# Layer 0 attention: Q, K and the negated maximum in two float32r parts, one product per head pair and key tile

## The chip, the cores and the metric

The kernel runs on one core of a Trainium2 chip. The metric is the device time of one execution in microseconds (us), lower is better. In the profile PE is the matrix engine (TensorE), PEld its loading of the stationary operand, DVE the vector engine, ACT the scalar engine, POOL the GpSimd engine and SP the engine whose queue issues most transfers. A "product" below is one matmul instruction.

## The reference

Two transformer layers follow each other; the second reads the first one's result. Only the attention of layer 0 is changed. It has 32 heads of 8 elements on 8 key/value heads, 2 batches of 1024 tokens, and a causal mask:

```
q = rope(x @ Wq + bq)      # 32 heads, 8 elements each
k = rope(x @ Wk + bk)      # 8 heads, each used by 4 query heads
v = x @ Wv + bv
scores = einsum('bhqd,bhkd->bhqk', q, k) / sqrt(8)
scores = where(kpos > qpos, -inf, scores)
out = (softmax(scores) @ v) @ Wo + bo
```

Everything is float32. The feed-forward net of layer 0 (8-bit arithmetic), then a windowed attention and a feed-forward net with ternary weights in layer 1 complete the program.

## The kernel before

**Tiling.** A query tile (b, i) is 128 tokens of batch b; there are 16 of them, done in the order (0,0) to (0,7), then (1,7) down to (1,0). Heads are split in two halves e = 0, 1: half 0 lives on partitions from 0, half 1 on partitions from 64, and the products of the two halves are issued as a pair, one right after the other.

**Float32 by bfloat16 parts.** Each q and each k is cut into three bfloat16 parts (`split`, lines 821 to 846: ACT rounds, DVE or POOL subtracts, twice). Of the nine pairs of parts, eight are stacked along the contraction, 8 pairs times 8 elements = 64 rows (`qmain`, `kmain`); the ninth pair stands with three rows for the parts of the negated maximum in a second stack of 35 rows (`qlast`, `klast`). In the trace, `k0` of batch 0 appears as plain `k`. The parts are written to a scratch in DRAM (`qscr`, `kscr`) and read back row by row into the stacks: `load_q` (line 940) issues eight transfers per query tile on SP, `stacks` (line 898) eight per chunk of 512 keys.

**Two passes over the scores.** For every query tile the kernel first finds the row maximum, and then computes the transposed scores with the maximum already subtracted:

- `max_unit` (lines 990 to 1034) multiplies the 64-row stacks (line 1016, tile `m`), up to 512 keys wide, adds the causal mask by bfloat16 products with an identity on 64 rows (line 988), and lets DVE reduce (line 1028, tile `mx`). Its three PSUM buffers hold one and a half such pairs. There are 304 units.
- `take_max` (lines 1036 to 1047) cuts the maximum into three parts on DVE, `turn_max` transposes them on PE, copies on ACT and sends them through DRAM (`mscr`) into the last three rows of the query stack.
- `weigh` (line 1075) forms the shifted scores `s` of a head pair and key tile with two products per half, the 64-row stack and the 35-row stack, accumulated:

```
for n, height in enumerate((HALF, EXTRA)):
    for e in range(2):
        rows = slice(HALF * e, HALF * e + height)
        nc.tensor.matmul(sc[e], kst[b][n][rows, ...], qst[b, i][n][rows, ...],
                         start=n == 0, stop=n == 1)
```

  ACT takes the exponential (line 1090). There are 288 such steps. `gather` (line 1110) multiplies the weights with v: four products of 9 columns in float32 (tile `acc`), once for every two steps.

**Order.** PE's order is the order of recording. The loop at the end of `attention0` counts slots: each slot records about one `max_unit` for a later tile, pieces of the feed-forward net of layer 0 and of other preparations as they come due, then one `weigh`, and after every second one the `gather` of the group before. The other engines' queues are ordered by the scheduler of the framework. The start is a chain: project K and Q for the first 512 tokens (`project`, line 853), cut them, write the scratch, load the stacks tile by tile (the next tile's write is issued behind the loads of the tile before), then the rest of the rope table and other inputs, all on SP. A fixed number of idle products (`keep_busy`, line 144) stands ahead of the first units. The parts of K for batch 1 share their memory with a staging area for the weights of the feed-forward net (`spare`), those of batch 0 later hold weights of layer 1.

## Time and profile before

Three executions took 1162.53, 1162.91 and 1166.25 us, a median of 1162.91 us. The profiled execution spans 1163.5 us from its first to its last instruction, 0.6 us from that median, so durations from the profile are set against the median as they are.

| stretch, us | what runs | PE busy | DVE busy | ACT busy | granted clock |
|---|---|---|---|---|---|
| 0 to 43 | first projections, cutting, first stacks | 29.68 | 27.78 | 9.15 | 0.92 |
| 43 to 94 | maxima of the first tiles, stacks of tiles 1 to 3 | 31.20 | 32.80 | 4.06 | 0.67 |
| 94 to 130 | first weighing | 30.54 | 28.32 | 15.50 | 0.81 |
| 130 to 400 | layer 0 | 226.59 | 232.48 | 145.01 | 0.91 |
| 400 to 770 | layer 0 | 329.85 | 299.91 | 257.40 | 0.96 |
| 770 to 1163.5 | layer 1 | 356.69 | 168.65 | 156.98 | 0.94 |

A stretch's busy time of an engine is the time in which at least one of its instructions was running by the trace. Products overlap each other, and the end of a product in the trace is modelled, so a busy PE is not a full PE. The chain of waits is the work followed back from the last instruction, each time to what released it.

### The profile page before, as it was taken

Reading aid. Unit: us, or ns where it says so; the run is one execution under the profiler, and the core shown is the slowest. Engines: PE = TensorE matmul, PEld = TensorE weight load, DVE = VectorE, ACT = ScalarE, POOL = GpSimd, SP = SyncE. Lnnn points to the kernel's source line nnn. Section 1 sums busy time; section 2 is a strip of 40 time slices with the busy share of each in tenths; the row PEclk is TensorE's granted clock in tenths of the full one; section 3 lists DMA queues with packets and bytes.
Section 4 is the critical chain, followed back from the end, with each engine's and each line's share of the span. In section 5 each row is a group of like instructions: output and inputs, shape, how many; then the busy total and the mean of one; then the engine's idle time right before and its main releaser. Section 6 shows DMA issues by size and latency. Waiting matters only on the chain.

```text
span 1163.5 us, 19952 instructions
## 1 busy us (share of the span) xinstructions
PE 1004.6 (86%) x7660; PEld 483.1 (42%) x7699; DVE 789.9 (68%) x1476; ACT 588.1 (51%) x1061; POOL 402.5 (35%) x440
## 2 busy tenths in 40 slices
PE   5758786888888989897989999896999999998897
PEld 2333331222332322232223333323567667666576
DVE  7467989889687998789897888703555544533431
ACT  2003461765356756576766777762463534533431
POOL 2007223424126121312133335545654635513400
PEclk9767896999799989998999999998999989989998
DMA  5432101000101010100001000006811332431200
GB/s 177 116 105 73 51 1 40 17 26 31 55 11 41 15 28 10 25 22 5 24 3 26 22 14 24 2 3 82 110 44 39 60 83 47 82 62 33 39 20 20
DMA packets 65928, 49.05 MB, mean 42 GB/s; under 512 B 20904, under 2 KB 59432, under 8 KB 65832
## 3 DMA queue, kind: packets, MB, share of 16 engines
q1 hardware_dynamic: 60632, 39.05, 15.1%
q0 software_dynamic: 4112, 8.26, 2.9%
q8 instruction: 60, 0.98, 0.4%
q10 hardware_dynamic: 1088, 0.46, 0.1%
q14 instruction: 36, 0.29, 0.1%
HBM read 34.12 MB, written 15.20 MB: 42 GB/s over the span
## 4 chain that ended last, share of the span: by engine, by line
PE 50%; DVE 28%; DMA 8%; ACT 6%; POOL 3%; issue 3%; SPq 2%; DVEq 0%; ACTq 0%; POOLq 0%
DVE mx L1028 14%; PE acc L1110 8%; PE s L1080 7%; PE f1gu L676 4%; PE sk L555 4%; PE f1o L715 3%; PE m L1016 3%; PE pqk L469 3%; PE sq L520 2%; DMA qscr<-ptq 2%; PE gu L305 2%; DMA qkv<-all 2%; ACT p L1090 2%; DMA qs<-mscr 1%; PE m L988 1%
## 5 line engine op out<-in xcount | busy, mean ns | idle before, releaser
L1028 DVE TENSOR_REDUCE mx<-m 128x1 f32<-128x512 f32 (+3 forms) x608 | 372.4, 653 | 95.8 <-PE m L1016 54.6
L1090 ACT ACTIVATE p<-s 128x512 f32<-128x512 f32 x576 | 307.2, 606 | 133.5 <-PE s L1080 131.0
L1110 PE MATMUL acc<-p,v 128*9 128x512 f32 x1152 | 171.0, 615 | 1.8 <-ACT p L1090 1.2
L1016 PE MATMUL m<-k,qmain 64*128 64x512 bf16 (+3 forms) x384 | 94.9, 359 | 52.9 <-DVE mx L1028 40.4
L1094 POOL TENSOR_SCALAR_AFFINE_SELECT p<-p 128x512 f32<-128x512 f32 x128 | 83.5, 675 | 160.8 <-ACT p L1090 160.5
L1016 PE MATMUL m<-kmain,qmain 64*128 64x512 bf16 (+3 forms) x384 | 83.1, 333 | 24.8 <-DVE mx L1028 22.7
L1016 PEld LDWEIGHTS <-qmain 64*128 64x128 bf16 x768 | 50.4, 100 | 81.8 <-issue 52.4
L988 PEld LDWEIGHTS <-ident_h 64*128 64x128 bf16 x832 | 45.6, 98 | 89.6 <-issue 67.0
L988 PE MATMUL m<-mask_q,ident_h 64*128 64x128 bf16 (+3 forms) x832 | 75.5, 223 | 2.4 <-DVE mx L1028 2.2
L1080 PE MATMUL s<-qmain,k 64*128 64x512 bf16 x288 | 68.1, 398 | 9.0 <-ACT ob L275 3.1
L1080 PE MATMUL s<-qmain,kmain 64*128 64x512 bf16 x288 | 64.2, 389 | 5.3 <-ACT p L1090 2.6
L1080 PE MATMUL s<-qlast,k 35*128 35x512 bf16 x288 | 63.9, 392 | 0.0
L1080 PEld LDWEIGHTS <-k 64*128 64x128 bf16 (+1 forms) x576 | 21.0, 95 | 99.0 <-issue 90.9
L1080 PE MATMUL s<-qlast,klast 35*128 35x512 bf16 x288 | 61.2, 387 | 0.0
L685 DVE SCALAR_TENSOR_TENSOR h<-h,f1gu 128x512 f32<-128x512 f32 x32 | 21.9, 686 | 49.2 <-ACT h L684 49.2
L676 PEld LDWEIGHTS <-wgu_bf 128*128 128x128 bf16 x384 | 38.1, 100 | 41.4 <-issue 4.7
L690 POOL TENSOR_TENSOR sq<-h 128x512 f32<-128x512 f32 x28 | 29.1, 1040 | 69.4 <-DVE h L686 68.0
L555 PE MATMUL sk<-qs,ks 25*128 25x128 f32 x512 | 45.5, 422 | 7.7 <-DMA qs<-mscr 7.7
L1153 POOL TENSOR_TENSOR x<-x,aos 128x256 f32<-128x256 f32 x16 | 11.9, 746 | 116.0 <-ACT aos L1152 116.0
L563 ACT ACTIVATE p<-sk 128x2048 f32<-128x2048 f32 x16 | 30.0, 1877 | 41.1 <-PE sk L555 41.1
L528 DVE TENSOR_REDUCE m<-sq 128x16 f32<-128x2048 f32 x16 | 36.6, 2286 | 20.9 <-PE sq L520 20.9
L153 POOL TENSOR_TENSOR hp<-hrest,hp 128x512 bf16<-128x512 f32 x32 | 37.0, 1157 | 35.4 <-ACT hp L152 35.4
(290 smaller groups left out, 1809.0 us busy)
## 6 DMA issues: line engine op xcount, KB each, us to landing
qmain<-qscr SPq DMA_DIRECT2D x64, 96.0 KB
qkv<-all SPq DMA_DIRECT2D x16, 384.0 KB
qscr<-ptq POOLq DMA_DIRECT2D x6, 384.0 KB, 4.2
x<-in_x SPq DMA_DIRECT2D x16, 128.0 KB
qmain<-qscr SPq DMA_DIRECT2D x32, 64.0 KB
qs<-qkv SPq DMA_DIRECT2D x16, 128.0 KB
ks<-qkv SPq DMA_DIRECT2D x16, 128.0 KB
vs<-qkv SPq DMA_DIRECT2D x16, 128.0 KB
```

The source lines that it names most:

```text
L153: engines[1].tensor_tensor(parts[2], r, parts[1], ALU.subtract)
L469: nc.tensor.matmul(pqk, x[k], wqk[:, k, :], start=(k == 0), stop=(k == 1))
L528: last(nc.vector.tensor_reduce(m, ps, AX.X, ALU.max, negate=True))
L555: nc.tensor.matmul(ps[:, s, r, :], columns(k, slice(S * s, S * s + HD + 9), 4 * b + r), columns(q, slice(S * s, S * s + HD + 9), 4 * b + r ...
L676: nc.tensor.matmul(ps[g], wgu_bf[:, k, g * HID + hc * P : g * HID + (hc + 1) * P], x_parts[n][m][:, k, :], start=(k == 0 and m == 0), stop ...
L988: nc.tensor.matmul(out[e][:, :, lo:], ident_h[rows, t, :], rhs.to_broadcast([HALF, out[e].shape[1], P - lo]), start=start and t == 0, stop ...
L1016: nc.tensor.matmul(sc[e][:, s * width : (s + 1) * width], qst[b, i][0][rows, p, :], kst[b][0][rows, lo // 512, p // 4, 0:width], start=not ...
L1028: reduced = nc.vector.tensor_reduce(mx[b, i][:, part, e, pairs[0] : pairs[0] + n], sc[e][:, : n * width].rearrange("p (s k) -> p s k", s=n ...
L1080: nc.tensor.matmul(sc[e], kst[b][n][rows, j // 4, u, j % 4 * P : (j % 4 + 1) * P], qst[b, i][n][rows, 4 * u : 4 * u + 4, :], start=n == 0, ...
L1090: nc.scalar.activation(p, sc[e], AF.Exp, scale=scale)
L1094: nc.gpsimd.affine_select(out=by_head, in_=by_head, compare_op=ALU.is_ge, fill=0.0, base=0, pattern=[[0, 4], [1, P]], channel_multiplier=-1,)
L1110: nc.tensor.matmul(acc[32 * s : 32 * s + HD0 + 1, :], vst[b][:, j, 4 * G + s, :], ps[s], start=(j == 0), stop=(j == i),)
```

## The change

Q and K are cut into two parts instead of three, kept in float32 and multiplied as float32r. The four pairs of parts make one stack of 4 times 8 = 32 rows; two rows more hold the parts of the negated maximum, so that `weigh` is one product of 34 rows per half, where it was two. `max_unit` uses the first 32 rows. A stack now takes four transfers instead of eight, with rows of 8 KB instead of 4 KB. The maximum is transposed in float32, cut by ACT (rounding) and DVE (rest, from PSUM), and sent as two rows. The tiles `qlast` and their clearing go; `klast` and its clearing give way to clearing both stacks of K with ones. Memory of K for batch 0 is taken over for layer 1 by new tiles (`take_k0`, called at the same place where the weights of layer 1 are loaded). A float32r product carries the loading of its stationary operand with it; a bfloat16 one has a separate instruction for that. The core of the diff:

```
 HALF = 64
-AUG = 32
-EXTRA = AUG + 3
+STACK = 32
+FULL = STACK + 2
...
-    k0 = [cp.tile([P, 2, KV0 // 2, 512], BF, tag=f"k0{n}", name=f"k0_{n}") for n in range(2)]
+    k0 = [cp.tile([P, KV0 // 2, 512], FR, tag=f"k0{c}", name=f"k0_{c}") for c in range(2)]
...
             def split(...):
-                def first():
-                    nc.scalar.copy(parts[:, 0], y)
-                    engine.tensor_tensor(r, y, parts[:, 0], ALU.subtract)
-                def second():
-                    nc.scalar.copy(parts[:, 1], r)
-                    last = engine.tensor_tensor(parts[:, 2], r, parts[:, 1], ALU.subtract)
+                def cut():
+                    parts, high, low = y
+                    nc.scalar.copy(high.bitcast(FR), low)
+                    last = engine.tensor_tensor(low, low, high, ALU.subtract)
...
             def prepare_k(b, c):
-                    engine.memset(kst[b][1].bitcast(F32), TWO_ONES)
+                    for n in range(2):
+                        (nc.gpsimd if b or n else nc.vector).memset(kst[b][n].bitcast(F32), 1.0)
...
-                        for n, row, pairs, part in ((0, 0, 3, 0), (0, 24, 3, 1), (0, 48, 2, 2), (1, 0, 1, 2)):
+                        for part in range(2):
+                            row = HALF * e + 2 * HD0 * part
...
             def load_q(b, i):
-                    for n, row, lo, hi in ((0, 0, 0, 3), (0, 24, 0, 3), (0, 48, 0, 2), (1, 0, 2, 3)):
+                    for n in range(2):
+                        row = HALF * e + 2 * HD0 * n
                         last_load[0] = nc.sync.dma_start(...)
...
             def max_unit(...):
-                        rows = slice(HALF * e, HALF * e + HALF)
+                        rows = slice(HALF * e, HALF * e + STACK)
                         nc.tensor.matmul(
                             sc[e][:, s * width : (s + 1) * width],
-                            qst[b, i][0][rows, p, :],
-                            kst[b][0][rows, lo // 512, p // 4, 0:width],
+                            qst[b, i][rows, p, :],
+                            kst[b][lo // 512][rows, p // 4, 0:width],
...
             def take_max(b, i):
-                nc.vector.tensor_copy(parts[:, 0], m)
-                nc.vector.tensor_tensor(r, m, parts[:, 0], ALU.subtract)
-                nc.vector.tensor_copy(parts[:, 1], r)
-                nc.vector.tensor_tensor(parts[:, 2], r, parts[:, 1], ALU.subtract)
...
             def turn_max(b, i, m):
-                nc.tensor.transpose(ps[: 3 * NH0], parts.rearrange("p a h -> p (a h)"), ident_bf)
-                nc.scalar.copy(mt, ps[: 3 * NH0])
+                nc.tensor.transpose(ps[:NH0], m, ident)
+                mt = pool.tile([NH0, 2, P], F32, tag="mt", name=f"mts{b}{i}", bufs=1)
+                nc.scalar.copy(mt[:, 0].bitcast(FR), ps[:NH0])
+                nc.vector.tensor_tensor(mt[:, 1], ps[:NH0], mt[:, 0], ALU.subtract)
...
             def weigh(b, i, u, j):
-                for n, height in enumerate((HALF, EXTRA)):
-                    for e in range(2):
-                        rows = slice(HALF * e, HALF * e + height)
-                        nc.tensor.matmul(
-                            sc[e],
-                            kst[b][n][rows, j // 4, u, j % 4 * P : (j % 4 + 1) * P],
-                            qst[b, i][n][rows, 4 * u : 4 * u + 4, :],
-                            start=n == 0,
-                            stop=n == 1,
-                        )
+                for e in range(2):
+                    rows = slice(HALF * e, HALF * e + FULL)
+                    nc.tensor.matmul(
+                        sc[e],
+                        kst[b][j // 4][rows, u, j % 4 * P : (j % 4 + 1) * P],
+                        qst[b, i][rows, 4 * u : 4 * u + 4, :],
+                        start=True,
+                        stop=True,
+                    )
...
-                for t in qlast:
-                    nc.vector.memset(t, 0.0)
```

## The prediction, made before the changed kernel was run

> **What bounds the kernel now.** I read the busy line first, then the table by stretch, the chain of waits of layer 0, and single products in the timeline.

> ```profile
> PE 1004.6 (86%) x7660; PEld 483.1 (42%) x7699; DVE 789.9 (68%) x1476; ACT 588.1 (51%) x1061; POOL 402.5 (35%) x440
> 130.00:400.00 270.00, 226.59 (x1505) 80.63 (x1513) 232.48 (x425) 145.01 (x276) 92.18 (x104) 0.91 0.10 28
> 400.00:770.00 370.00, 329.85 (x2597) 110.70 (x2609) 299.91 (x594) 257.40 (x497) 116.39 (x143) 0.96 0.06 16
> ```

> The last two lines are stretches of layer 0: span, then busy time of PE, PEld, DVE, ACT, POOL, then PE's granted clock. DVE is busy 86% of the first and 81% of the second, PE 84% and 89%: neither alone sets the end. The chain between 100 and 770 us says the same, and the waits say who waits for whom (total us, times, longest):

> ```profile
> by line: DVE mx L1028 25.2%; PE acc L1110 12.9%; PE s L1080 11.2%; PE m L1016 5.3%; PE gu L305 3.5%; ACT p L1090 2.8%; issue 2.7%; PE m L988 2.3%; PE ot L1125 1.6%; PE f0o L265 1.4%; DVE xn L195 1.2%; DVE fw L319 1.1%; DVE act L221 1.0%; PE
> PE m L1016 <- DVE mx L1028: 56.6, 89, 4.6
> DVE mx L1028 <- PE m L1016: 44.7, 40, 3.2
> ```

> PE's lines add up to some 43% of that chain (`s` 75 us of 670), DVE's maxima to 25%. The two wait for each other in turn. So I let 45% of a change in PE's work here reach the end; the ends are 25% (DVE holds) and 80% (PE holds).

> Before the weighing begins at 93.4 us the chain is of another kind:

> ```profile
> by line: DMA qscr<-ptq 30.3%; SPq L940 21.7%; DMA rope<-in_rope 14.7%; DMA qmain<-qscr 11.7%; issue 4.8%; POOL restq L829 4.5%; POOL ptq L833 4.1%; DVE q010y L864 2.5%; POOL q011y L868 2.3%; POOL q010y L868 2.2%; ACT ptq L832 2.2%; POOL qsc
> 73.41 0.70 SPq L940
> 74.11 0.05 issue
> 74.17 0.63 SPq L940
> ...
> 78.42 8.39 DMA rope<-in_rope
> ```

> SP issues the stack transfers of the first tiles one by one, 0.43 to 0.70 us each, and the rest of the rope table comes behind them.

> What PE pays inside a step shows in the timeline (start, duration, then the product):

> ```profile
> 604.43 1.04 PE L1110 MATMUL acc<-p,v 128*9 128x512 f32 x8
> 605.41 0.39 PE L1080 MATMUL s<-qmain,kmain 64*128 64x512 bf16 x2
> 605.64 0.38 PE L1080 MATMUL s<-qlast,klast 35*128 35x512 bf16 x2
> 605.86 0.38 PE L1016 MATMUL m<-kmain,qmain 64*128 64x512 bf16 x2
> ```

> The two halves of a bfloat16 pair run together; pairs of 512 columns follow each other 0.22 us apart, from `s` to `s` and from `s` to `m`, which are all on 64 rows. Where the shape of the array's tile changes there is more: `acc` to `s` takes 0.98 against 2 x 0.43 = 0.86 for its two records, and `s` to `acc` (another place, 369.99 to 370.30) 0.31 against 0.22. A change of shape costs 0.09 to 0.12; I take 0.095.

> **The head, 40 to 94 us.** 20 of the issues of L940 between 40.5 and 78.4 us are on the chain, 13 us. Transfers per tile fall from eight to four: -6.5 us; two more microseconds of the same issues lie before 40.5, another -1.1. Cutting into two parts leaves out one ACT copy (0.63) and one subtraction (0.69 on DVE, about 1.16 on POOL) where a cut is on the chain, at the start and at L829 to L833: -2. Sum -9.6; I take **-9**. The bytes of a stack go from 590 to 524 KB, those of a scratch write from 98 to 131 KB per half tile, so the landings (`qmain` 6.69, `qscr` 6.2 to 6.3 us on the chain) may give some back. One write a third longer costs about 2 us and there are three on the chain, which bounds the gain at -4; if the landings follow the number of transfers it is -13. The projections and cuts of later chunks are covered by the maxima, and cost nothing in the sum; without cover their saved copies would bring 12 x 0.62 = 7 us.

> **PE from 94 to 780 us, stream.** `weigh` loses one pair per step: 288 x 0.217 = -63 us. How fast a float32r product streams no row shows. The ends are 0.22 per pair of 512 columns (bfloat16) and 0.86 (the float32 rows, two records of 0.43). [...]

> **Change of shape.** `m` now uses 32 rows while `s` and the mask stay on 64, so by the order of PE's instructions the shape changes 1008 times in the attention of layer 0, against 500: `s` to `m` 221 more, `m` to mask 195, mask to `m` 67, others 25. 508 x 0.095 = **+48 us**. [...]

> **Loading of the stationary operand.** A bfloat16 load takes 0.093 us and hides, a float32 one 0.19:

> ```profile
> L1080 PEld LDWEIGHTS <-kmain x288: 92/93/148, 499.0 to 778.1; 64*128 64x128 bf16 x144
> L1149 PEld LDWEIGHTS ao<-wo,oT x64: 186/190/243, 134.7 to 786.6; 128*128 128x128 f32 x64
> L1149 PE MATMUL ao<-wo,oT x64: 379/379/483, 134.7 to 786.8; 128*128 128x256 f32 x64
> ```

> (minimum, median and maximum in ns.) Behind a product of its own shape the float32 load hides too: equal float32 records of the projections (L853, 366 to 369 us) follow each other every 0.43 us. The first `ao` after a change of shape takes 483 instead of 379, so +0.10 is exposed; the first bfloat16 `s` takes 386 instead of 372, +0.01. About 310 `m` and 210 `s` pairs will stand first after a change. At 0.09 this is 520 x 0.09 = **+47 us**; at the bfloat16 row +5, with the whole 0.19 in sight +99. I take 0.09, as the operand is float32 by its bytes. Some 64 pairs of only 128 columns stream for less than a load takes: +3 to +10, say +5.

> PE's sum: -63 + 48 + 47 + 5 = +37; with the 45% it is **+16** (+9 at 25%, +29 at 80%).

> [...] No run here shows a float32r product yet.

> **DVE and the rest.** `take_max` loses four small operations of 0.10 us on the chain, 16 times: -7. One subtraction per tile from PSUM (+4 at some 0.25) comes in, behind PE's transpose and ACT's copy. While DVE stands at it, the maxima queued behind wait, and PE with three PSUM buffers behind them: 16 x 0.2 to 0.3 = +3 to +5. The three subtractions fewer on DVE and the `qlast` clearing (4 x 0.91) lie outside the chain. Sum **-1**. Layer 1 issues the same instructions: 0.

> **Sum.** 1163.5 - 9 + 16 - 1 = 1169.5 by the profile, 0.6 less against the median: **1169**.

> **The rivals.**
> 1. Loads hidden, on the other side (faster). If the float32r load hides as the bfloat16 one does (+5 instead of +47, narrow pairs 0), PE's sum is -63 + 48 + 5 = -10, times 0.45 = -5; with -9 and -1 the time is 1148. It decides at an exposed load of 0.05 us: there PE's sum is -63 + 48 + 26 + 5 = +16, of which 7 arrive against the 10 of the head and DVE. For it: every load with a neighbour of its own shape hides now. Against it: the 483 of `ao`. Chance 0.30, 1143 to 1158.
> 2. float32r streams at half rate, 0.43 per pair of 512. The one product then costs what two did (-63 becomes 0), and the 384 pairs of `m`, at 0.16 us more on average (some are 128 to 384 columns wide), add 61: PE +161, times 0.45 = +72, about 1225 with the head's gain. At the 80% end it passes 1280. For it: four bytes per element instead of two. Chance 0.13, 1195 to 1260.
> 3. DVE holds the end and the landings take half the head: 37 x 0.25 = +9, head -7, DVE -1: about 1163. For it: the 25.2% of `mx`. Chance 0.08.
> 4. The change does not do what it says: excluded by the order of the instructions, where `s` has 576 products instead of 1152.

> **How the numbers follow.** The forecast's case has chance 0.49, with its own range 1159 to 1186 (loads between 0.05 and 0.15, share between 25% and 60%). A difference of 0.3%, 3.5 us, is about what a measurement of this kernel can tell from none. Faster: rival 1 (0.30), and 0.05 from the edges of the forecast and of rival 3. Same: 0.10 (rival 3 mostly, and the forecast's low edge). Slower: the rest of the forecast (0.42) and rival 2, 0.55. The range from 1144 to 1200 holds the forecast, rival 3 and most of rival 1 and leaves out most of rival 2 and the low edge of rival 1, together under 0.2.

> **What would show it.** Right: pairs of `s` or `m` in one shape 0.22 us apart; 0.09 or more between `s` and `m` beyond the stream; the first pair after a change longer by 0.10; the rest of the rope table at 69 to 70 us instead of 78.4, weighing from 84 instead of 93.4; between 100 and 770 more PE on the chain than now. Wrong: the first pairs no longer than the others (rival 1), 0.43 between equal pairs (rival 2), or a head that begins to weigh later than 90.

## The result, and the profile after

The changed kernel takes 1277.6 us (median of four executions, 1263.0 to 1286.3) against 1164.6 us for the kernel before: a ratio of 1.094, with an interval of 1.087 to 1.100. Medians here and below are of all executions of a kernel, ratios of its fast ones alone (an execution more than 1.5% above the kernel's fastest is left out of them), so the two can differ by some 0.3%. The profiled execution is the longest of the four (1286.28 us, span 1284.5), so its rows are read for their shares and clocks and not for the last per cent of the time.

The busy line of the page:

```profile
PE 1184.3 (92%) x7084; PEld 570.5 (44%) x7123; DVE 778.5 (61%) x1421; ACT 588.1 (46%) x1049; POOL 391.2 (30%) x433
```

PE has 576 products fewer than before and is busy 180 us longer. DVE's, ACT's and POOL's work is the same or a little less. The table by stretch shows why (span, busy times of PE, PEld, DVE, ACT and POOL, then PE's granted clock, DMA share and GB/s):

```profile
130.00:400.00 270.00, 250.67 (x1066) 97.89 (x1069) 188.77 (x339) 111.60 (x209) 64.53 (x75) 0.68 0.09 22
400.00:770.00 370.00, 354.02 (x1775) 128.64 (x1776) 262.86 (x487) 214.69 (x404) 86.44 (x110) 0.77 0.09 17
```

In the same stretches the clock was 0.91 and 0.96 before; now it is 0.68 and 0.77. In 270 us PE ends 1066 products instead of 1505, and DVE, which had been busy 86% of the first stretch, waits. The chain of waits between 100 and 770 us:

```profile
by line: PE acc L1108 19.8%; PE m L1019 18.7%; PE s L1078 14.1%; DVE mx L1031 10.8%; PE gu L308 5.1%; PE m L991 4.8%; PE ot L1123 2.3%; PE f0o L268 2.0%; PE ao L1147 1.8%; ACT p L1088 1.8%; DVE fw L325 1.4%; issue 1.3%; PE q111p L848 1.0%; 
```

PE's lines shown here add up to some 70%, and with its smaller ones to 76% of the chain (44% before, counted in the same way); DVE's maxima have fallen from 25.2% to 10.8%. Even `acc`, which the change does not touch, has grown from 12.9% to 19.8%. One part of the second stretch, cut where the clock changes:

```profile
430.10:542.70 112.60, 110.27 (x412) 35.92 (x414) 68.83 (x121) 49.23 (x89) 13.31 (x17) 0.50 0.04 7
542.70:570.00 27.30, 25.87 (x163) 8.98 (x155) 21.09 (x40) 18.89 (x36) 2.67 (x5) 1.00 0.11 30
```

The clock records of the two kernels have two values, 0.50 and 1.00, and here the clock stays at 0.50 for 112.6 us in a row, with PE "busy" for 98% of it. Per microsecond in which PE is busy it ends 3.7 products at half clock and 6.3 at full clock. So the question is why a PE that is never idle is not given its clock.

The waits of PEld name something else that is new:

```profile
PEld s L1078 <- issue: 116.5, 119, 1.7
...
PEld m L1019 <- DVE mx L1031: 78.1, 147, 6.6
```

Before, it was the product `m` that waited for DVE (56.6 us, 89 times), and no load of `m` did; the trace has those bfloat16 loads under their stationary operand alone (`<-qmain`). The float32r loads it has under the names of the whole product (`m<-k,qst`), and such a load waits for the PSUM buffer that DVE has to free, 147 times and 78.1 us, and starts only then.

The time is lost between the first and the last `s`: 684.9 us before (93.4 to 778.3), 807.8 now (87.7 to 895.5). What follows the last `s` takes 385.2 and 389.0 us.

### The profile page after: what moved, and what is told of

Its sections match the earlier page's. It is cut to its first block, busy times and chain, and to the rows that moved or that the text cites. A ratio compares the mean times of both kernels' runs of the same rounds, so it can differ in the third digit from the quotient of the medians.

```text
span 1284.5 us, 18436 instructions
## 1 busy us (share of the span) xinstructions
PE 1184.3 (92%) x7084; PEld 570.5 (44%) x7123; DVE 778.5 (61%) x1421; ACT 588.1 (46%) x1049; POOL 391.2 (30%) x433
## 4 chain that ended last, share of the span: by engine, by line
PE 72%; DVE 14%; ACT 5%; DMA 4%; issue 2%; POOL 2%; SPq 0%; DVEq 0%; ACTq 0%; POOLq 0%
PE acc L1108 13%; PE m L1019 12%; PE s L1078 9%; DVE mx L1031 7%; PE f1gu L679 4%; PE m L991 3%; PE sk L558 3%; PE f1o L718 3%; PE pqk L472 3%; PE gu L308 3%; PE sq L523 2%; PE ot L1123 2%; DMA qs<-mscr 1%; ACT p L1088 1%; PE ao L1147 1%
## 5 line engine op out<-in xcount | busy, mean ns | idle before, releaser
L1019 PE MATMUL m<-k,qst 32*128 32x512 f32 (+3 forms) x768 | 249.0, 528 | 37.7 <-DVE mx L1031 31.9
L1108 PE MATMUL acc<-p,v 128*9 128x512 f32 x1152 | 204.6, 754 | 0.6 <-ACT o L1117 0.3
L1019 PEld LDWEIGHTS m<-k,qst 32*128 32x128 f32 x768 | 108.3, 222 | 167.1 <-DVE mx L1031 88.1
L1078 PE MATMUL s<-qst,k 34*128 34x512 f32 x576 | 177.1, 582 | 2.7 <-ACT p L1088 1.7
L1078 PEld LDWEIGHTS s<-qst,k 34*128 34x128 f32 x576 | 68.4, 219 | 204.6 <-issue 139.5
L558 PE MATMUL sk<-qs,ks 25*128 25x128 f32 x512 | 44.7, 423 | 8.7 <-DMA qs<-mscr 8.6
L991 PEld LDWEIGHTS <-ident_h 64*128 64x128 bf16 x832 | 25.9, 99 | 54.4 <-issue 48.7
L679 PE MATMUL f1gu<-xparts,wgu_bf 128*128 128x512 bf16 x179 | 45.6, 403 | 1.0 <-issue 0.4
L472 PE MATMUL pqk<-after_k,xnT 128*128 128x512 f32 x64 | 38.8, 737 | 8.4 <-ACT all L495 8.0
L718 PE MATMUL f1o<-after_k,hp 128*128 128x256 bf16 x384 | 45.5, 277 | 1.0 <-DVE x L726 0.5
L308 PE MATMUL gu<-xq,wg 128*128 128x512 bf16 x112 | 41.9, 476 | 3.7 <-issue 1.7
```

What stands on the lines that cost most here:

```text
L308: nc.tensor.matmul(ps, wg[:, u, k, hc * P : (hc + 1) * P], xq[:, k, :], start=(k == 0), stop=(k == 1))
L472: nc.tensor.matmul(pqk, x[k], wqk[:, k, :], start=(k == 0), stop=(k == 1))
L558: nc.tensor.matmul(ps[:, s, r, :], columns(k, slice(S * s, S * s + HD + 9), 4 * b + r), columns(q, slice(S * s, S * s + HD + 9), 4 * b + r ...
L679: nc.tensor.matmul(ps[g], wgu_bf[:, k, g * HID + hc * P : g * HID + (hc + 1) * P], x_parts[n][m][:, k, :], start=(k == 0 and m == 0), stop ...
L718: nc.tensor.matmul(po, hs[hc][:, m, i * P : (i + 1) * P], wp[:, hc, :], start=(hc == 0 and m == 0), stop=(hc == NHC - 1 and m == 2),)
L991: nc.tensor.matmul(out[e][:, :, lo:], ident_h[rows, t, :], rhs.to_broadcast([HALF, out[e].shape[1], P - lo]), start=start and t == 0, stop ...
```

## The experiments

### The changed kernel without its changes of shape (wide)

```
-                        rows = slice(HALF * e, HALF * e + STACK)      # m
+                        rows = slice(HALF * e, HALF * e + FULL)
+ load_q: rows 32 and 33 of the query stack are set to zero by one more transfer per half
```

> The changed kernel, with the maxima's products (m) on the first 34 rows instead of 32, so that m, mask and s all use array tiles of 64 rows; two transfers per query tile set the two extra rows to zero beforehand. The order, the float32r operands and the columns are those of the changed kernel; only the changes of shape go back to about 500. Theory G (the granted clock falls because float32r loads and changes of shape leave PE standing too often for the clock to come back): s to m falls from 0.43 to 0.22 to 0.33 us at full clock, the mean granted clock between 130 and 770 us rises from 0.73 to 0.88 or more, time 1130 to 1180 us. Theory P (float32r products themselves bring the clock down, whatever their shape): the clock stays at or below 0.78 and the time at or above 1230. Theory L (the loads are exposed in any shape): spacing stays at 0.43, time within 1240 to 1280.

1220.3 us, ratio 1.045 (1.041 to 1.049), clock 0.81. Half of the loss is gone and half stays; none of the theories named in the expectation had put it there. From `s` to the next `m` it is 0.335 us at full clock. The load of a float32r product takes 0.183 us (minimum, median and maximum in ns), where the bfloat16 one of the kernel before took 0.093:

```profile
L1087 PEld LDWEIGHTS s<-qst,k x576: 182/183/335, 84.7 to 829.7; 34*128 34x128 f32 x192
```

### The kernel before with a change of shape (narrow)

```
-                        rows = slice(HALF * e, HALF * e + HALF)       # m
+                        rows = slice(HALF * e, HALF * e + HALF // 2)
```

> The kernel before (bfloat16), with m on 32 of its 64 rows, which leaves the smaller pairs of parts out of the maximum (the maximum is only a shift, the softmax stays the same). It adds the changes of shape of the changed kernel (500 to some 1008) and no float32r. Theory G: changes of shape alone cost 508 x 0.095 = 48 us of PE, and the clock between 130 and 770 us falls from 0.94 to 0.80 to 0.90; time 1190 to 1235. Theory P: the clock stays at 0.92 to 0.95, and 45% of 48 us arrive, time 1175 to 1190. If bfloat16 loads hide across a change of shape too: below 1175.

1201.3 us, ratio 1.032 (1.026 to 1.038), clock 0.91. No float32r, and still 36 us slower with a clock below that of before: P is not the whole cause. G's range for the time held, the clock fell less than it said.

These two and the two kernels make a square, and the timeline prices its sides. Of narrow, wide and the changed kernel, in this order, at full clock:

```profile
603.13 0.38 PE L1080 MATMUL s<-qlast,klast 35*128 35x512 bf16 x2
603.44 0.39 PE L1016 MATMUL m<-kmain,qmain 32*128 32x512 bf16 x2
```

```profile
603.58 0.49 PE L1087 MATMUL s<-qst,k 34*128 34x512 f32 x2
603.91 0.39 PE L1028 MATMUL m<-k,qst 34*128 34x512 f32 x2
604.14 0.40 PE L1087 MATMUL s<-qst,k 34*128 34x512 f32 x2
```

```profile
558.26 0.49 PE L1078 MATMUL s<-qst,k 34*128 34x512 f32 x2
558.68 0.50 PE L1019 MATMUL m<-k,qst 32*128 32x512 f32 x2
```

Over all such neighbours at full clock the median from `s` to `m` is 0.220 us before, 0.313 in narrow (a change of shape, +0.093), 0.335 in wide (a float32r load in sight, +0.115) and 0.427 in the changed kernel (+0.207, the sum of the two). In the third line of wide the next `s` follows `m` in 0.23 us and lasts 0.40, not 0.49: here float32r streams about as fast as bfloat16 did (0.22), and its load is hidden behind a product of the same shape with no wait in between. That is rare: at full clock 96% of the `s` and 98% of the `m` of 512 columns in the changed kernel show their load (over 0.45 us instead of 0.38 to 0.40); in wide 90% and 34%.

### Bursts of idle products (burst)

```
-                wait_busy({0: 55, 4 + 1: 10}.get(at, 0))
+                wait_busy({0: 55, 4 + 1: 10}.get(at, 16 if at >= 40 and at % 30 == 10 else 0))
```

> The changed kernel, with 16 idle bfloat16 products of 512 columns in a row (3.4 us at full clock, 6.8 at half) ahead of every 30th unit of the maxima, ten times in all: pure extra work on PE of 35 to 68 us. Theory G: each burst gives a dense window and brings the clock back to full; the mean granted clock between 130 and 770 us rises from 0.73 to 0.82 or more, and the time stays at or falls below that of the changed kernel (1225 to 1280) in spite of the extra work. Theory P: the clock does not come back or falls again at once; time 1310 to 1345.

1300.5 us, ratio 1.115 (1.112 to 1.118), clock 0.79. A miss for both. The clock rose, but only three of the ten bursts began while it was at half (at 151.7, 320.8 and 776.7 us); each of these was followed by full clock, for 30.7, 3.4 and 30.7 us. The other seven began at full clock already.

### The removed product alone, in bfloat16 (short)

```
-                for n, height in enumerate((HALF, EXTRA)):
+                for n, height in enumerate((HALF,)):
```

> The kernel before (bfloat16), with one product per half in weigh: the 35-row stack is left out, so the maximum is not subtracted and the smallest pair of parts is missing. It prices the removed product alone: PE loses 288 x 0.217 = 63 us with no float32r and no new change of shape. By the share of 45% the time falls by 28 to about 1135 (1115 to 1150). If the removed products were what kept the clock up (a denser PE), the clock between 130 and 770 us falls below 0.90 and the time is 1150 to 1180.

1145.4 us, ratio 0.982 (0.980 to 0.985), clock 0.93. This kernel leaves out the subtraction of the maximum and the smallest pair of parts. The removed product is worth 19.5 us, 31% of the 63 us that PE saves, and the clock does not need it.

### More work against the clock (fill)

```
+                for e in range(2):
+                    rows = slice(HALF * e, HALF * e + HALF)
+                    idle = ident_bf[rows, None, :].to_broadcast([HALF, 4, P])
+                    nc.tensor.matmul(
+                        sc[e].rearrange("p (h q) -> p h q", h=4), ident_h[rows, 0, :], idle, start=True, stop=True
+                    )
                 for e in range(2):
                     rows = slice(HALF * e, HALF * e + FULL)             # s of run wide
```

> The kernel of run wide with one idle bfloat16 pair of 512 columns on 64 rows ahead of each float32r pair of weigh, into the same PSUM tiles, which the real products then overwrite: pure extra work, 288 pairs of 0.22 us at full clock. It takes the place of the 0.11 us for which the float32r pair that stands first after a change of shape stands still, so PE's steps grow by 288 x 0.11 = 32 us net at full clock, while PE's stream gets denser. Theory G (the clock comes back only after a dense window): the mean granted clock between 130 and 770 us rises from 0.815 to 0.88 or more and the time falls below that of wide (1220), to 1175 to 1210, in spite of more work. Theory W (work alone counts, the clock is only a symptom): 1235 to 1255.

1175.8 us, ratio 1.013 (1.010 to 1.016), clock 0.91. With 288 idle pairs more than wide it is 44 us faster:

```profile
130.00:770.00 640.00, 584.46 (x3999) 251.51 (x4016) 515.71 (x947) 389.80 (x744) 192.57 (x231) 0.91 0.10 21
```

against, in wide,

```profile
130.00:770.00 640.00, 576.23 (x3232) 235.71 (x3246) 498.92 (x911) 365.25 (x694) 176.49 (x208) 0.81 0.10 21
```

So the clock is a cause and no symptom: DVE, ACT and POOL all get more done in the same 640 us. But the idle products have 64 rows, and that left open whether the time in which something streams or the rows in use count.

### Only s in float32r (mixed)

```
-                            qst[b, i][rows, p, :],
-                            kst[b][lo // 512][rows, p // 4, 0:width],
+                            qst[b, i].bitcast(BF)[rows, p, 1::2],
+                            kst[b][lo // 512].bitcast(BF)[rows, p // 4, 1 : 2 * width : 2],
```

> The kernel of run wide with m (the maxima) read as bfloat16 from the upper halves of the float32 parts (stride 2), so that only s is float32r; the maximum is then rougher, but it is only a shift, and the softmax stays the same. No new change of shape, bfloat16 loads for m apart from their products. If float32r loads that wait with their product are what costs, m's part of it goes: PE -63 + 288 x 0.11 = -31 us at full clock, clock 0.87 to 0.93 between 130 and 770 us, time 1145 to 1185. If s alone brings the clock down: clock below 0.85, time 1195 to 1220.

1202.4 us, ratio 1.035 (1.032 to 1.038), clock 0.81. The float32r loads of `m` are gone (PEld is busy 207.96 us between 130 and 770 us, in wide 235.71) and the clock is that of wide. So the loads of `m` don't explain the clock; `s` is float32r here as in wide, where 90% of its products show their load, and wide64 below settles these. This, with the next run, is where theory R comes from.

### One stack of six bfloat16 pairs (six)

```
+STACK = 48
+FULL = STACK + 3
-                        for n, row, pairs, part in ((0, 0, 3, 0), (0, 24, 3, 1), (0, 48, 2, 2), (1, 0, 1, 2)):
+                        for n, row, pairs, part in ((0, 0, 3, 0), (0, 24, 2, 1), (0, 40, 1, 2)):
-                    for n, row, lo, hi in ((0, 0, 0, 3), (0, 24, 0, 3), (0, 48, 0, 2), (1, 0, 2, 3)):
+                    for n, row, lo, hi in ((0, 0, 0, 3), (0, 24, 0, 2), (0, 40, 0, 1)):
-                for n, height in enumerate((HALF, EXTRA)):
+                for n, height in enumerate((FULL,)):
```

> The kernel before (three bfloat16 parts), with only the six pairs of parts whose orders add up to 2 or less: 48 rows, and the three rows of the maximum behind them, one stack of 51 rows, one product per half in weigh; three transfers per half and tile instead of four. It has what the change wanted (one product, fewer transfers) without float32r and without a new change of shape. Run short priced the removed product at -19.5 us; the head adds some -3 to -4 (two of eight issues per tile): 1138 to 1148 us. If the gain of short came from the transfer of the maximum or other work it left out: 1150 to 1165.

1152.9 us, ratio 0.992 (0.990 to 0.995), clock 0.89: a miss, 5 us above what was expected. In this kernel `m` uses 48 rows and `s` 51. It begins to weigh 10.2 us earlier than short (83.05 against 93.27 us), and is yet slower: from the first to the last `s` it takes 680.8 us, short 664.6. The two differ there in rows, 48 and 51 against 64, and in the clock, 0.89 against 0.93; short also never has to wait for the maxima.

### What the clock records say

In the traces of the kernel before and of the changed kernel the clock keeps its value for whole multiples of 3.41 us, the last record aside (33 of them make the 112.6 us above). For each such stretch, from 95 to 900 us, I took the time in which products stream (512 bfloat16 columns in 0.427 us at half clock, as equal products follow each other in the traces, in half of that, 0.213, at full clock, where they follow each other every 0.215, and twice that for float32, whose equal records in the projections follow each other every 0.43), either as time covered or weighted by the share of the array in use (rows out of 128; for `acc` 32 columns out of 128 as well), and asked what clock came next. All thirteen kernels together:

| streaming by share of the array | at half: back to full next | at full: still full next |
|---|---|---|
| below 0.3 | 0 of 145 | 13 of 161 |
| 0.3 to 0.4 | 0 of 48 | 122 of 204 |
| 0.4 to 0.6 | 3 of 133 | 913 of 914 |
| 0.6 to 0.7 | 20 of 174 | 472 of 472 |
| 0.7 to 0.8 | 75 of 129 | 292 of 292 |
| 0.8 and more | 137 of 137 | 256 of 256 |

Over the first twelve of these kernels one bound on the share of the array, 0.75, sorts 94% of the stretches at half clock rightly; the best bound on covered time, 0.85, sorts 88%. In these records a stretch at full clock was followed by half clock in 230 of 365 cases below a share of 0.4 and in 1 of 1934 above it; one at half clock was followed by full clock in 23 of 500 cases below 0.7, in 75 of 129 from 0.7 to 0.8, and in all 137 above. From 0.4 to 0.7 the clock mostly stayed what it was. This is an ordering of records and not yet a cause; the next runs change the rows alone.

### Fewer rows, nothing else (few)

```
-                        rows = slice(HALF * e, HALF * e + HALF)       # m
+                        rows = slice(HALF * e, HALF * e + HALF // 2 + 1)
```

> The kernel before (bfloat16), with m on 33 of its 64 rows: one row more than in run narrow, so the array's tile stays at 64 rows and no change of shape is added. The smaller pairs of parts are left out of the maximum, which is only a shift. Stream, loads and order are those of the kernel before; only the number of rows in use is lower. Theory R (the clock is granted by how many rows stream, not only by how much of the time a product streams): the clock between 130 and 770 us falls from 0.94 to 0.84 to 0.92 and the time rises by 8 to 30 us, 1170 to 1192. Theory G (only the time in which something streams counts): clock 0.94, time within 5 us of the kernel before. Run narrow minus this run is what the changes of shape cost.

1172.4 us, ratio 1.007 (1.004 to 1.010), clock 0.92. A kernel with the same products, streams and loads is 9 us slower for using fewer rows. It is the low end of what R said, and outside G's 5 us. Narrow minus few, 29 us, is what the changes of shape cost in bfloat16: 62% of 508 x 0.093 us.

### More rows, nothing else (wide64)

```
-                        rows = slice(HALF * e, HALF * e + FULL)       # m and s
+                        rows = slice(HALF * e, HALF * e + HALF)
+ the four query stacks are tiles of their own, cleared once; rows 32 and 33 are set to zero from the fifth query tile on
```

> The kernel of run wide with m and s on 64 rows instead of 34; rows 34 to 63 of the query stack are zero, those of the key stack one. Same result, same order, loads and stream times; only more rows in use. Theory R: the clock between 130 and 770 us rises from 0.815 to 0.88 or more and the time falls from 1220 to 1165 to 1200. Theory G: clock 0.80 to 0.83, time 1210 to 1225.

1164.2 us, ratio 1.000 (0.998 to 1.002), clock 0.92:

```profile
130.00:770.00 640.00, 566.93 (x3563) 237.58 (x3562) 521.08 (x959) 398.15 (x767) 203.53 (x244) 0.92 0.10 22
```

That is 1 us less than R's range. Thirty rows of zeros per stack are worth 56 us: 3563 products in 640 us instead of 3232. PE is not busy longer than in wide (566.93 us against 576.23), and the loads are as exposed as there: at full clock 0.337 us from `s` to `m`, and 91% of the `s` of 512 columns show their load. So neither the time in which PE is busy (G), nor float32r by itself (P), nor the exposed loads hold the clock of wide down. Zeros add nothing to any product; what sets the two kernels apart is the rows in use, and the clock is 0.92 against 0.81. Other contents than zeros were not tried.

### The best of both (six64)

```
+FULL = HALF                                                        # s and m of run six on 64 rows
+                qst[b, i] = [qlast[used % len(qlast)]]                # cleared once
+                if used >= len(qlast):
+                    for e in range(2):
+                        nc.sync.dma_start(out=qst[b, i][0][HALF * e + STACK : HALF * e + MAX3]..., in_=zeros)
```

> The kernel of run six with its one stack filled up with zero rows to 64 (48 rows of pairs, 3 of the maximum, 13 of zeros), m and s on all 64, the rows of the maximum set to zero ahead of m by two small transfers per tile from the fifth tile on. Same stream times and order. Theory R: the clock between 130 and 770 us rises from 0.89 (six) to 0.92 to 0.95 (as in run short) and the time falls from 1153 to 1134 to 1146. Theory G: within 4 us of six.

1137.8 us, ratio 0.979 (0.974 to 0.984), clock 0.94. It is the fastest kernel here, 2.1% under the kernel before. Its four times lie 18 us apart (1126.8 to 1145.0) and the profile is of the fastest; all four are below those of six. Of six and six64:

```profile
130.00:770.00 640.00, 544.29 (x3579) 174.50 (x3592) 524.46 (x1003) 402.77 (x780) 216.57 (x257) 0.89 0.07 17
130.00:770.00 640.00, 537.73 (x3664) 178.06 (x3663) 526.41 (x1000) 408.91 (x793) 226.50 (x266) 0.94 0.08 18
```

From the first to the last `s` it takes 664.9 us, as short did, though it waits for the maxima.

### The changed kernel with s alone on 64 rows (pad_s)

```
                 for e in range(2):
-                    rows = slice(HALF * e, HALF * e + FULL)             # s
+                    rows = slice(HALF * e, HALF * e + HALF)
+ four query stacks of their own, cleared once
```

> The changed kernel itself, with s alone on 64 rows instead of 34 (rows 34 to 63 of the query stack zero, of the key stack one); m stays on 32 rows, with all its changes of shape and exposed loads. Same result, order, loads and stream times. Theory R: the clock between 130 and 770 us rises from 0.73 to 0.79 to 0.86 and the time falls from 1277 to 1215 to 1255. Theory G: within 10 us of the changed kernel, clock 0.71 to 0.75.

1247.0 us, ratio 1.070 (1.067 to 1.074), clock 0.82. Zeros in `s` alone give back 31 us of the changed kernel's 113; `m` stays on 32 rows, with its changes of shape, and `s` to `m` still takes 0.43 us. Of the changed kernel and of pad_s:

```profile
130.00:770.00 640.00, 604.69 (x2833) 226.53 (x2845) 451.63 (x824) 326.28 (x612) 150.97 (x184) 0.73 0.09 19
130.00:770.00 640.00, 597.16 (x3056) 228.31 (x3071) 479.71 (x880) 348.95 (x660) 161.96 (x195) 0.82 0.09 20
```

## Why the prediction was wrong

**The loss, step by step.** From the kernel before to wide64, the whole change with its rows kept at 64, the time is the same (1163 and 1164 us): the shorter head and the removed product pay for the exposed loads. Taking the rows from 64 to 34 costs 56 us (wide), and going to 32 for `m`, with 508 changes of shape, another 57 (1277.6). In that last step rows and shape change together; by narrow minus few the shapes account for about half of it.

**The step that failed** is one that the prediction does not have: it took the granted clock as given. Its table of stretches had the clock in the column beside the busy times, 0.91 and 0.96, and every term after that was priced by rows at full clock. By its own steps with the measured sizes, PE's sum would be -63 + 47 + 75 + 5 = +64 and 45% of it +29; with -9 and -1 that is an estimate of 1182 us. The other 95 us or so lie in a clock of 0.73 instead of 0.94. The runs give nearly the same split without the 45%: wide64 shows that head, removed product and exposed loads come to nothing together, the changes of shape cost 29 us where the clock hardly moves (narrow minus few), and about 84 of the 113 us are left for the clock. Both splits are estimates. That PE is busy did not keep its clock: it was busy 110.27 of 112.60 us at half clock. In these runs the clock followed the rows in use: 0.81 in wide, 0.92 in wide64.

**The loads.** The term was 520 x 0.09 = 47 us. Measured, a load in sight costs 0.115, and nearly all of the 288 + 384 pairs have one: 672 x 0.115 x 0.97 = 75. The count left out the waits of the float32r load for DVE (the 147 above), which expose it as a change of shape does: in wide one half of an `m` pair without such a wait takes 0.39 us, the other half, behind a wait, 0.49 (604.37 and 605.08 us). The 483 against 379 of `ao` gave the right size, 0.10.

**The changes of shape** were right: 0.093 measured in narrow against 0.095. **The stream** was right: 0.23 us from `m` to `s` in wide against the 0.22 that the forecast has. No row of the kernel before shows a float32r product; the 0.22 there is that of bfloat16 pairs, and to expect it of float32r was the author's estimate. The rival of half the rate is out.

**The share** of 45% is not one number: 31% of what PE saved arrived in short and 62% of what it paid in narrow minus few, and once PE is slow it holds 76% of the chain. The two bounds of 25% and 80% were a hint that a larger PE term would not keep the share of the smaller one.

**The head** was right in its place and too large: the rest of the rope table is issued at 69.1 us (69 to 70 said, 78.4 before); the first `s` comes at 87.7 (84 said, 93.4 before). From 43 to 94 us PE is now busy 46.70 us, where it was 31.20, at about the same clock (0.65, 0.67 before), and the last thing ahead of the first `s` is a projection on PE; that PE's longer maxima hold the head is argued from this and not tested. **DVE's** term of -1 was not measured on its own.

**The rivals.** In wide a float32r load was hidden behind a neighbour of the same shape with no wait (0.40 us instead of 0.49, at 604.14 us); `m` mostly stands so, and 34% of its products show their load, but of `s` 90% do. The forecast's direction was right, and its size was 4 of 113 us. The direction was not luck, as the changes of shape by themselves make the kernel slower (narrow), but most of the 113 us came from what the forecast did not have.

**What stays open.** By what exactly the clock is granted: between shares of 0.6 and 0.8 my count does not decide, and whether columns in use count as rows do was not tried.

## What to carry to other kernels

Read the granted clock as a quantity that the change can move (0.94 to 0.73 here): if a change makes PE's products use fewer rows (0.92 in wide64, 0.81 in wide), or makes PE stand between them (0.92 in few, 0.91 in narrow), price the stretch at half clock as well (3.7 products per busy microsecond here instead of 6.3), and look at whether anything in it is dense enough to win the clock back, as stretches with a share of 0.8 and more were in these records. Where a stack is shorter than its tile and the clock is not full, try filling it up with zeros: it cost no stream time here (0.34 us from `s` to `m` in wide64 as in wide) and was worth 56, 31 and 15 us (wide, the changed kernel, six). The float32r products saved 576 products here, but their loads stood in the waits (147 times and 78.1 us for `m` behind DVE), so one stack of bfloat16 parts, cut to the pairs that matter and filled up to the tile, gave what the change was after (1137.8 us).

## What the runs showed of the hardware that was not expected

- Rows of zeros raised the granted clock: 0.81 in wide, 0.92 in wide64 with 64 rows instead of 34, the products, their shapes and their exposed loads alike.
- By the count above the clock was lost mostly below a share of 0.4 of the array (230 of 231 times) and won back mostly above 0.7 (212 of 235 times). Two kernels with nearly the same work differed by 5% in time (wide 1220.3 us, wide64 1164.2), and adding 288 idle pairs made one 44 us faster.
- A float32r load took 0.183 us where a bfloat16 one took 0.093, showed as 0.115 where it was exposed, and added to the 0.093 of a change of shape: 0.220, 0.313, 0.335 and 0.427 us from `s` to `m`.
